# A gated attention and feed-forward block on one core: another order of the outer products, gated products through PSUM, stores by four, earlier inner factors of k and v, queued layernorms

## The chip, the cores and the metric

The kernel runs on one core of one Trainium2 chip, as one program with one launch. The metric is device time in microseconds. Three runs of the kernel before took 1561.82, 1562.58 and 1565.77 us; the median is 1562.58 us. One more execution was profiled. All shares and durations below are from it.

## The reference

Eight sequences of 512 tokens with 512 features go through one block in float32:

```python
xn = layernorm(x)                                    # (8, 512, 512)
q, k, v = xn @ Wq.T + bq, xn @ Wk.T + bk, xn @ Wv.T + bv
kv = cumsum((elu(k) + 1) * v, axis=tokens)
s  = ((elu(q) + 1) * kv * 32 ** -0.5) @ Wo.T + bo    # elementwise linear attention
h  = fwht(xn * SU_ug) / 64                           # normalized Walsh-Hadamard, 512
h  = silu(h @ W_gate.T * (Wscale_gate * 64)) * (h @ W_up.T * (Wscale_up * 64))   # 2048 wide
f  = (fwht(h * SU_dp) / 64) @ W_down.T * (Wscale_dp * 64)
out = x + s * silu(f)
```

The scan over tokens is elementwise per feature. The rest is matrix products, with the Hadamard transforms folded into the weights once, at the start.

## The kernel before

**Products.** Every large product is made by a fast scheme with seven products in place of eight for a matrix cut in two by two. The seven are called `P1` to `P7`; their factors are sums and differences of blocks of the tokens and of the weights. Most stages use it twice, one inside the other: an outer product is one of seven, and is itself made of seven inner ones. Inner products are accumulated in PSUM banks with the tags `px`, `py`, `pz` (3, 1 and 2 banks; two more have the tag `t`). After each step VectorE or ScalarE reads a partial sum out (`sa`, `sb`, `sc`) or adds a result (L737, L739, L743, L768, L770). TensorE goes on in the same bank only after the read.

**Pairs and stages.** The eight sequences are four pairs, `p` = 0 to 3. A pair has these stages, in order: attention (in pairs 0 and 1 from projected k, v and q; in pairs 2 and 3 k and v are made by outer products, `by_blocks`, L991), four hidden units `u` = 0 to 3 (`hidden_unit`, L1024), the output projection after unit 0 (`project_out`), the first half of the down product after unit 1, and its second half (`down`) after unit 3, with the gating, the residual and the output. The first half of down is `down` in pair 0 and seven outer products (`down_by_blocks`, L1093) in pairs 1 to 3. In time: pair 0 to about 451 us, pair 1 to 837, pair 2 to 1196, pair 3 to the end. Unit 1 and the outer products of down meet at about 640, 1010 and 1370 us.

**Hidden units.** One unit is seven outer products in the order `IN_TURN` = P1, P5, P6, P2, P7, P3, P4, each with its own weight tile `w_gu` from DRAM. Four results come out, numbered (a, s): (1,1) after the fifth outer product, (0,0), (0,1) and (1,0) later. `gated` turns a result into a gated product: ScalarE makes silu of the gate, an elementwise engine multiplies by the other lane, and subtractions make the factors that the down product needs (`ho`, seven places). In even units GpSimd does all of that, 1024 elements a partition at a time. In odd units (the ones before a down product) VectorE does it for (0,1) and (1,0). Subtractions are L1027, products L1035.

**Outer products of down.** For outer product `n` the function `factors` makes three inner factors from blocks of `ho` of units 0 and 1 (L1120 to L1122), and `last_factor` a fourth (L1129). GpSimd makes them, but for the second outer product, whose three are VectorE's. The order is `IN_TURN`. The results (`ra`, `rv`, `ru1`, `rr`, `u3`) are combined by `plus` (L1174). Each of the four is then transposed by VectorE in two pieces (L1148), into room in unit 1's `ho` that is no longer needed, and stored to DRAM in eight transfers of 64 KB (L1142). The order of weight loads follows the order of use; a list of all of them is written before the loop.

**What sets the order of work.** The program is written in steps of one inner factor. `at(n, fn)` puts work into an agenda, n steps from now; `advance` runs the agenda. `later(us, fn)` puts work into a queue called `idle`; `pace(ins, us)` takes work worth `us` from it whenever a result has been added, and places it behind that instruction on its engine. If a stage passes a time of zero, nothing is taken there. `catch_up` empties the queue. The framework then orders all instructions of each engine by its own plan. Every engine runs its own list in order. All loads and stores go through SP's queue, also in order. Weights are asked for three tiles ahead, from a pool of four.

**Buffers.** The pool `xin` has one buffer (tag `x`). It takes in turn a raw sequence for its layernorm, inner factors of down (`factors_down`, seven times in pair 1, every 13 steps from step 7) and the even sequence of the next pair's tokens (`squares`). Six buffers `t8` hold results, fetched sums and, in pair 1, the inner factors of k and v (`factors_kv`: four times two loads, seven stores and four additions or subtractions on VectorE), which begin after unit 1, in steps 2, 14, 26 and 38.

**Layernorms.** `normalized(b)` loads a sequence into `xin`, normalizes it and stores it. For b = 2 its 9 pieces are put into the queue. For b = 3 to 7 they are written as one block, at a lower priority (L148 statistics, L151 to L153 the root, L155 the scaling). In the profile, batch 4 is normalized at 551 to 573 us, 5 at 585 to 596, 6 at 823 to 832, 7 at 850 to 861.

Of the kernel before, what the change touches and what calls it, by code (L numbers as in the profile page):

```python
# [22 lines left out]
def kernel(  # L23
# [27 lines left out]
    nc = tc.nc  # L51
# [139 lines left out]
    def normalized(b):  # L191

        xt = load_x(b)
        d = dram.tile([L, D], F32, tag=f"d_x_{b}", name=f"d_x_{b}")
        kept[f"x_{b}"] = d

        def store():
            nc.sync.dma_start(d.rearrange("(n p) d -> p n d", p=P), xt)

        if b > 2:  # L200
            layernorm(b, xt)
            store()
# [241 lines left out]
    def factors_kv(m, lo, hi):  # L444
# [5 lines left out]
        t = t8.tile([P, 4, 4, P], F32, tag="t", name=f"f_{m}_{lo}")  # L450
# [573 lines left out]
    def hidden_unit(p, u, xo, ho, get_w, last, time=0):  # L1024
# [4 lines left out]
        def gated(t, a, s):  # L1029
            eng = nc.vector if last and a != s else nc.gpsimd  # L1030
            g, v = (t[:, :, lane].rearrange("p m q t -> p m (q t)") for lane in range(2))
            for m in range(2):
                nc.scalar.activation(g[:, m], g[:, m], AF.Silu, scale=col("w_gate", u + m * NU + a * NG))  # L1033
# [59 lines left out]
    def down_by_blocks(p, hos, get_w):  # L1093
# [15 lines left out]
        places = {}  # L1109

        def factors(n):
            o = IN_TURN[n]
            eng = nc.vector if n == 1 else nc.gpsimd
# [3 lines left out]
            else:  # L1117
                x, y = (block(0, q, IN_TURN[n - 3]) for q in range(2))
            b = block
            eng.tensor_tensor(x, b(1, 1, o), b(0, 1, o), ALU.subtract)  # L1120
            eng.tensor_tensor(b(0, 1, o), b(0, 1, o), b(0, 0, o), ALU.subtract)
            eng.tensor_tensor(y, b(1, 1, o), b(0, 1, o), ALU.subtract)  # L1122
# [4 lines left out]
        def last_factor(n):  # L1127
            b = block(1, 0, IN_TURN[n])
            nc.gpsimd.tensor_tensor(b, b, places[n][P6], ALU.subtract)  # L1129

        stored = []

        def turned(t, a, s):
            o = (P5, P1)[len(stored) // 2]
            z = h1[:, len(stored) % 2, o : o + 2]
            stored.append((a, s))

            def store():
                d = ds[s].rearrange("(i t) (c j f) -> j t c i f", t=32, j=4, f=32)
                for m in range(2):  # L1140
                    for j in range(4):
                        nc.sync.dma_start(  # L1142
                            d[j][:, 2 * a + m],
                            z[32 * j : 32 * j + 32, m].rearrange("p (i f) -> p i f", f=32),
                        )

            for m in range(2):
                at(1 + 2 * m, lambda m=m: nc.vector.transpose(z[:, m], t[:, m, 0].rearrange("p q t -> p (q t)")))  # L1148
            at(4, store)

        def outer(n, out, add=None, done=None):
            i = IN_TURN[n]
# [5 lines left out]
        u3, f0 = halves("u3")  # L1158
# [4 lines left out]
        at(3, lambda: factors(2))  # L1163
# [6 lines left out]
        ra, rv, ru1, rr, u3 = (result(t) for t in (ra, rv, ru1, rr, u3))  # L1170
# [5 lines left out]
        def with_u1():  # L1176
            plus(u3, ru1, rv)

        def with_r():
            plus(rv, rv, rr)  # L1180
# [184 lines left out]
    for p in range(B // 2):  # L1365
# [5 lines left out]
        for u in range(NU):  # L1371
# [7 lines left out]
            if u % 2:  # L1379
                if p and u == 1:  # L1380
                    queue += [(p, "dl", i) for i in IN_TURN]
# [112 lines left out]
    for p in range(B // 2):  # L1494
        if p:
            catch_up()
            inner_tokens(xo)
            if p == 1:
                for n, i in enumerate(IN_TURN):
                    at(7 + 13 * n, lambda i=i: factors_down(i))  # L1500
            co = hop.tile([P, 2, 7, L], F32, tag="h", name=f"co_{p}")
# [3 lines left out]
        for u in range(NU):  # L1505
# [9 lines left out]
            else:  # L1515
# [8 lines left out]
                hidden_unit(p, u, xo, ho, get_w, u % 2 == 1, 1.1 if p > 1 and u == 0 else 0)  # L1524
# [8 lines left out]
            if u == 1:  # L1533
# [12 lines left out]
        flush()  # L1546
        ds = [fetch(f"d_{p}_{s}") for s in range(2)]
# [59 lines left out]
```

## Time and profile before

| | |
|---|---|
| median of three runs | 1562.58 us (1561.82 to 1565.77) |
| profiled execution: its time, and its span from the first to the last instruction | 1559.57 us, 1557.8 us |
| TensorE busy | 1507.0 us, 97% of the span, 6008 matmuls |
| VectorE busy | 1143.8 us, 73% |
| ScalarE busy | 408.0 us, 26% |
| GpSimd busy | 472.0 us, 30% |
| granted TensorE clock, mean | 0.994 |
| DMA | 307.31 MB, mean 197 GB/s |

PE is TensorE, PEld its weight loads, DVE VectorE, ACT ScalarE, POOL GpSimd, SP the engine that issues the DMAs; "SPq" is its sequencer. Lnnn is a line of the kernel. A group or a row has the line, the engine, the operation, output and input by the program's names, the shape, and how many. In square brackets stand the idle time of the engine before it and what ended that idle time. The ends of matmuls are modelled and overlap, so a busy TensorE is not one at its peak. Starts are in us from the start of the span.

### The profile page before, as it was taken

How to read it: one execution, taken by the hardware profiler on the slowest of the kernel's cores; microseconds unless marked ns; L12 is line 12 of the kernel's file. 1: busy time of each engine (PE TensorE's matmuls, PEld its weight loads, DVE VectorE, ACT ScalarE, POOL GpSimd, SP SyncE). 2: the span in 40 equal slices, each digit the busy share in tenths (PEclk: the TensorE clock that was granted, in tenths of full speed). 3: DMA queues.
4: the chain of work that ended last, by engine and by line, in shares of the span. 5: the costliest groups of instructions: out<-in, count | busy, mean ns of one | idle time of the engine just before them, and what ended most of it. 6: DMA issues, size and time to landing. Idle time of an engine off the chain costs nothing.

```text
span 1557.8 us, 16546 instructions
## 1 busy us (share of the span) xinstructions
PE 1507.0 (97%) x6008; PEld 1139.2 (73%) x6008; DVE 1143.8 (73%) x1743; ACT 408.0 (26%) x668; POOL 472.0 (30%) x263
## 2 busy tenths in 40 slices
PE   7998999999999989888999999999999999989998
PEld 3446446748864778777886888878887788878887
DVE  8999787569756876876677796676675697576673
ACT  4462341232134321201214332111211432111211
POOL 1000000001211261843622227471622118381731
PEclk9999999999999999999999999999999999999999
DMA  9346878798956656698586643548475342538472
GB/s 278 94 141 175 260 269 239 226 306 286 267 173 212 235 179 213 199 271 235 178 248 228 188 150 135 180 127 197 168 230 189 121 161 97 200 136 197 157 259 83
DMA packets 274481, 307.31 MB, mean 197 GB/s; under 512 B 108640, under 2 KB 227680, under 8 KB 271712
## 3 DMA queue, kind: packets, MB, share of 16 engines
q1 hardware_dynamic: 274256, 306.22, 63.5%
q8 instruction: 47, 0.77, 0.2%
q14 instruction: 34, 0.28, 0.1%
q10 hardware_dynamic: 144, 0.03, 0.0%
HBM read 217.35 MB, written 88.87 MB: 197 GB/s over the span
## 4 chain that ended last, share of the span: by engine, by line
PE 71%; DVE 14%; DMA 4%; POOL 3%; SPq 3%; issue 2%; ACT 2%; POOLq 0%; DVEq 0%; ACTq 0%
PE px_gu L713 13%; PE px_dn L616 7%; PE pz_gu L713 6%; PE py_gu L713 3%; PE pz_dn L616 3%; PE px_q L540 3%; PE px_kv L713 3%; PE px_o L616 3%; PE px_gate L540 2%; PE px_dl L722 2%; PE py_dn L616 2%; PE px_up L540 2%; PE pz_o L616 2%; PE pz_kv L713 2%; PE px_k L540 1%
## 5 line engine op out<-in xcount | busy, mean ns | idle before, releaser
L713 PE MATMUL px_gu<-xo,w_gu 128*128 128x256 f32 x1456 | 350.6, 381 | 11.2 <-DMA w_gu<-d_gu 6.8
L713 PEld LDWEIGHTS px_gu<-xo,w_gu 128*128 128x128 f32 x1456 | 275.7, 190 | 57.2 <-DMA w_gu<-d_gu 6.3
L1005 POOL TENSOR_TENSOR u_gu<-u_gu,v_gu 128x1024 f32<-128x1024 f32 x26 | 61.2, 2373 | 630.7 <-DVE u_gu L770 569.7
L713 PE MATMUL pz_gu<-xo,w_gu 128*128 128x256 f32 x728 | 189.9, 384 | 1.9 <-DVE u_gu L743 1.8
L713 PEld LDWEIGHTS pz_gu<-xo,w_gu 128*128 128x128 f32 x728 | 139.2, 192 | 23.3 <-DVE u_gu L743 3.8
L616 PE MATMUL px_dn<-w_down,ho 128*128 128x256 f32 x640 | 143.0, 379 | 1.8 <-DVE ho L94 1.8
L616 PEld LDWEIGHTS px_dn<-w_down,ho 128*128 128x128 f32 x640 | 121.5, 190 | 20.3 <-DVE ho L94 2.2
L713 PE MATMUL py_gu<-xo,w_gu 128*128 128x256 f32 x364 | 95.1, 383 | 0.0
L1062 POOL TENSOR_TENSOR s<-s,d 128x512 f32<-128x512 f32 x30 | 39.4, 1312 | 166.4 <-ACT d L1061 166.4
L722 PE MATMUL px_dl<-ho,w_dl 128*128 128x256 f32 x300 | 75.1, 386 | 3.0 <-ACT sc_dl L737 1.4
L713 PEld LDWEIGHTS py_gu<-xo,w_gu 128*128 128x128 f32 x364 | 69.5, 191 | 9.6 <-DVE v_gu L743 0.2
L616 PE MATMUL pz_dn<-w_down,ho 128*128 128x256 f32 x304 | 69.1, 379 | 0.6 <-DVE u L556 0.6
L722 PEld LDWEIGHTS px_dl<-ho,w_dl 128*128 128x128 f32 x300 | 57.2, 193 | 14.0 <-ACT sc_dl L737 2.6
L1009 POOL TENSOR_TENSOR v_gu<-v_gu,r_gu 128x1024 f32<-128x1024 f32 x26 | 60.9, 2363 | 18.2 <-DVE r_gu L770 18.2
L616 PEld LDWEIGHTS pz_dn<-w_down,ho 128*128 128x128 f32 x304 | 57.5, 190 | 10.3 <-issue 1.2
L540 PE MATMUL px_q<-xo,w_q 128*128 128x512 f32 x128 | 59.8, 593 | 0.0
L616 PE MATMUL px_o<-w_o,co 128*128 128x256 f32 x256 | 59.2, 380 | 0.3 <-DVE sa_o L627 0.3
L1061 ACT ACTIVATE d<-d 128x512 f32<-128x512 f32 x31 | 19.5, 630 | 148.8 <-DVE d L631 126.4
L1027 POOL TENSOR_TENSOR ho<-ho 128x1024 f32<-128x1024 f32 x24 | 56.6, 2367 | 1.4
L737 ACT COPY sa_gu<-px_gu 128x512 f32<-128x512 f32 x26 | 15.1, 581 | 157.9 <-PE px_gu L713 129.1
L1033 ACT ACTIVATE a_gu<-a_gu,cols_sb 128x512 f32<-128x512 f32 x26 | 18.6, 720 | 141.6 <-DVE a_gu L770 140.2
L616 PEld LDWEIGHTS px_o<-w_o,co 128*128 128x128 f32 x256 | 48.3, 190 | 8.9 <-issue 1.0
(373 smaller groups left out, 2833.9 us busy)
## 6 DMA issues: line engine op xcount, KB each, us to landing
w_gu<-d_gu SPq DMA_DIRECT2D x91, 896.0 KB, 4.7
w_dl<-d_dl SPq DMA_DIRECT2D x21, 896.0 KB, 4.5
w_down<-d_down SPq DMA_DIRECT2D x35, 512.0 KB, 5.3
w_kv<-d_kv SPq DMA_DIRECT2D x14, 896.0 KB, 4.7
d_s<-o SPq DMA_DIRECT2D x8, 1024.0 KB, 6.2
d<-d_d SPq DMA_DIRECT2D x8, 1024.0 KB, 6.1
s<-d_s SPq DMA_DIRECT2D x8, 1024.0 KB, 8.3
y<-in_x_dram SPq DMA_DIRECT2D x8, 1024.0 KB, 6.8
```

The lines of the kernel that those rows point to most:

```text
L540: nc.tensor.matmul(p.rearrange("p a t -> p (a t)") if len(r.shape) == 2 else p, ws[k][:, i, :], r, start=(first and k == 0), stop=(k == n ...
L616: nc.tensor.matmul(p[:, c], t[:, (2 * g + c) * P : (2 * g + c + 1) * P], ws[i](k), start=(first and k == 0 and c == cs[0]), stop=(k == n - ...
L713: nc.tensor.matmul(p[:, lane], w[:, lane, i, :], x[:, i, :], start=(first and lane == 0), stop=True, skip_group_check=True,)
L722: nc.tensor.matmul(p[:, 0], w[:, k, i, :], x(k, i), start=(first and k == 0), stop=(k == 1), skip_group_check=True,)
L737: nc.scalar.copy(s, px)
L1005: nc.gpsimd.tensor_tensor(r[:, m], ru1[:, m], rv[:, m], ALU.add)
L1009: nc.gpsimd.tensor_tensor(rv[:, m], rv[:, m], rr[:, m], ALU.add)
L1027: eng.tensor_tensor(ho[:, :, c], ho[:, :, a], ho[:, :, b], ALU.subtract)
L1033: nc.scalar.activation(g[:, m], g[:, m], AF.Silu, scale=col("w_gate", u + m * NU + a * NG))
L1061: nc.scalar.activation(d, d, AF.Silu)
L1062: (nc.vector if final and (a, s) == (1, 0) else nc.gpsimd).tensor_tensor(r, r, d, ALU.mult)
```

## The change

It has six parts.

- **Gated products of odd units.** For (0,1) and (1,0) ScalarE writes silu of the gate into a PSUM bank of the tag `t`, in two pieces of 512 elements. VectorE multiplies there, and forms P5 and P7 (or P2) from the PSUM piece. GpSimd does the two remaining subtractions, P6 and P4.
- **Order of the outer products of down**: P1, P3, P6, P5, P7, P2, P4 in place of `IN_TURN`. All `factors` are GpSimd's, all `last_factor` VectorE's. The result `r3` takes the place of `u3`: it is the second outer product, and two sums are added to it later.
- **Turned results.** The eight transposes of a pair go into the queue. Each sequence is stored once, in four transfers of 256 KB, when both its results are there.
- **Inner factors of k and v** begin in steps 100, 114, 128 and 142 of pair 1, which is in unit 0 and `project_out`, and use the buffer `xin`.
- **Layernorms** of b = 4 to 7 are put into the queue, from step 12 after unit 1 or 2; b = 3 is still a block.
- **Pacing.** Hidden units of pairs 1 to 3 take work from the queue (1.1 us for a result), but for unit 0 of pair 1. Before, only unit 0 of pairs 2 and 3 did. At the end of a pair the queue is emptied.

```diff
-        if b > 2:
+        if b == 3:
             layernorm(b, xt)
...
-        t = t8.tile([P, 4, 4, P], F32, tag="t", name=f"f_{m}_{lo}")
+        t = xin.tile([P, 3, 7, P], F32, tag="x", name=f"f_{m}_{lo}")
+        t = t.rearrange("p c s e -> p (c s e)")[:, : 16 * P].rearrange("p (a s e) -> p a s e", a=4, s=4)
...
         def gated(t, a, s):
-            eng = nc.vector if last and a != s else nc.gpsimd
+            eng = nc.gpsimd
             g, v = (t[:, :, lane].rearrange("p m q t -> p m (q t)") for lane in range(2))
+            if last and a != s:
+                bs = []
+                for m in range(2):
+                    b = bank("t", f"g_{p}_{u}_{a}_{m}", 1)[:, 0]
+                    nc.scalar.activation(b, g[:, m], AF.Silu, scale=col("w_gate", u + m * NU + a * NG))
+                    if s:
+                        nc.vector.tensor_tensor(b, b, v[:, m], ALU.mult)
+                        nc.vector.tensor_tensor(ho[:, m, P5], b, ho[:, m, P1], ALU.subtract)
+                        bs.append(b)
+                    else:
+                        nc.vector.tensor_tensor(ho[:, m, P2], b, v[:, m], ALU.mult)
+                if s:
+                    sub(eng, P6, P3, P5)
+                    for m in range(2):
+                        nc.vector.tensor_tensor(ho[:, m, P7], ho[:, m, P3], bs[m], ALU.subtract)
+                else:
+                    sub(eng, P4, P2, P6)
+                return
...
+        ORDER = (P1, P3, P6, P5, P7, P2, P4)
...
-            eng = nc.vector if n == 1 else nc.gpsimd
...
-            eng.tensor_tensor(x, b(1, 1, o), b(0, 1, o), ALU.subtract)
+            nc.gpsimd.tensor_tensor(x, b(1, 1, o), b(0, 1, o), ALU.subtract)
...
         def last_factor(n):
-            b = block(1, 0, IN_TURN[n])
-            nc.gpsimd.tensor_tensor(b, b, places[n][P6], ALU.subtract)
+            b = block(1, 0, ORDER[n])
+            nc.vector.tensor_tensor(b, b, places[n][P6], ALU.subtract)
...
         def turned(t, a, s):
...
-            for m in range(2):
-                at(1 + 2 * m, lambda m=m: nc.vector.transpose(z[:, m], t[:, m, 0].rearrange("p q t -> p (q t)")))
-            at(4, store)
+            z = h1[:, s, 2 * a : 2 * a + 2]
+            for m in range(2):
+                later(0.7, nc.vector.transpose, z[:, m], t[:, m, 0].rearrange("p q t -> p (q t)"))
+
+        def store(s):
+            z = h1[:, s, 0:4].rearrange("p c (i f) -> p c i f", f=32)
+            d = ds[s].rearrange("(i t) (c j f) -> j t c i f", t=32, j=4, f=32)
+            for j in range(4):
+                nc.sync.dma_start(d[j], z[32 * j : 32 * j + 32])
...
-        def with_u1():
-            plus(u3, ru1, rv)
...
+        def with_v():
+            plus(r3, r3, rv)
+            plus(r3, r3, ru1)
+
+        def with_a():
+            turned(r3, 0, 1)
             turned(rv, 1, 1)
+            later(0.0, store, 1)
+            turned(ra, 0, 0)
+
+        def with_c():
+            turned(ru1, 1, 0)
+            later(0.0, store, 0)
...
         outer(0, ra)
-        outer(1, rv)
-        outer(2, ru1, ra, with_u1)
-        outer(3, ra, ra, lambda: turned(ra, 0, 0))
-        outer(4, rr, ru1, with_r)
-        outer(5, u3, u3, lambda: turned(u3, 0, 1))
-        outer(6, ru1, rr, lambda: turned(ru1, 1, 0))
+        outer(1, r3)
+        outer(2, ru1, ra)
+        outer(3, rv, None, with_v)
+        outer(4, rr, ru1, lambda: plus(rv, rv, rr))
+        outer(5, ra, ra, with_a)
+        outer(6, ru1, rr, with_c)
...
+                for i, (m, lo, hi) in enumerate((("k", 0, 4), ("k", 4, 7), ("v", 0, 4), ("v", 4, 7))):
+                    at(100 + 14 * i, lambda m=m, lo=lo, hi=hi: factors_kv(m, lo, hi))
...
-                hidden_unit(p, u, xo, ho, get_w, u % 2 == 1, 1.1 if p > 1 and u == 0 else 0)
+                hidden_unit(p, u, xo, ho, get_w, u % 2 == 1, 1.1 if p and (p > 1 or u) else 0)
...
-                if p == 1:
-                    for i, (m, lo, hi) in enumerate((("k", 0, 4), ("k", 4, 7), ("v", 0, 4), ("v", 4, 7))):
-                        at(2 + 12 * i, lambda m=m, lo=lo, hi=hi: factors_kv(m, lo, hi))
...
+        if p:
+            catch_up()
```

More of the change, by code (lines that the diff above doesn't have):

```diff
@@ L1109, in down_by_blocks @@
         places = {}
+        ORDER = (P1, P3, P6, P5, P7, P2, P4)
         def factors(n):
-            o = IN_TURN[n]
-            eng = nc.vector if n == 1 else nc.gpsimd
+            o = ORDER[n]
             if n < 3:
@@ L1117, in factors @@
             else:
-                x, y = (block(0, q, IN_TURN[n - 3]) for q in range(2))
+                x, y = (block(0, q, ORDER[n - 3]) for q in range(2))
             b = block
-            eng.tensor_tensor(x, b(1, 1, o), b(0, 1, o), ALU.subtract)
-            eng.tensor_tensor(b(0, 1, o), b(0, 1, o), b(0, 0, o), ALU.subtract)
-            eng.tensor_tensor(y, b(1, 1, o), b(0, 1, o), ALU.subtract)
+            nc.gpsimd.tensor_tensor(x, b(1, 1, o), b(0, 1, o), ALU.subtract)
+            nc.gpsimd.tensor_tensor(b(0, 1, o), b(0, 1, o), b(0, 0, o), ALU.subtract)
+            nc.gpsimd.tensor_tensor(y, b(1, 1, o), b(0, 1, o), ALU.subtract)
             places[n] = {
@@ L1127, in last_factor @@
         def last_factor(n):
-            b = block(1, 0, IN_TURN[n])
-            nc.gpsimd.tensor_tensor(b, b, places[n][P6], ALU.subtract)
-        stored = []
+            b = block(1, 0, ORDER[n])
+            nc.vector.tensor_tensor(b, b, places[n][P6], ALU.subtract)
         def turned(t, a, s):
[L1134 to L1139, printed above, removed]
-                for m in range(2):
[L1141 to L1145, printed above, removed]
-            for m in range(2):
-                at(1 + 2 * m, lambda m=m: nc.vector.transpose(z[:, m], t[:, m, 0].rearrange("p q t -> p (q t)")))
-            at(4, store)
+            z = h1[:, s, 2 * a : 2 * a + 2]
+            for m in range(2):
+                later(0.7, nc.vector.transpose, z[:, m], t[:, m, 0].rearrange("p q t -> p (q t)"))
[4 more added lines that the diff above has]
+                nc.sync.dma_start(d[j], z[32 * j : 32 * j + 32])
         def outer(n, out, add=None, done=None):
-            i = IN_TURN[n]
+            i = ORDER[n]
             w = get_w("dl", i)
@@ L1156, in outer @@
             )
-        u3, f0 = halves("u3")
+        r3, f0 = halves("r3")
         room.append(f0)
@@ L1162, in down_by_blocks @@
         at(0, lambda: factors(1))
-        at(3, lambda: factors(2))
+        at(2, lambda: factors(2))
         for n in range(3, 7):
@@ L1169, in down_by_blocks @@
         ru1, rr = halves("u1")
-        ra, rv, ru1, rr, u3 = (result(t) for t in (ra, rv, ru1, rr, u3))
+        ra, rv, ru1, rr, r3 = (result(t) for t in (ra, rv, ru1, rr, r3))
         def plus(o, a, b):
@@ L1174, in plus @@
             nc.vector.tensor_tensor(o, a, b, ALU.add)
-        def with_u1():
-            plus(u3, ru1, rv)
-        def with_r():
-            plus(rv, rv, rr)
-            turned(rv, 1, 1)
-        outer(0, ra)
-        outer(1, rv)
-        outer(2, ru1, ra, with_u1)
-        outer(3, ra, ra, lambda: turned(ra, 0, 0))
-        outer(4, rr, ru1, with_r)
-        outer(5, u3, u3, lambda: turned(u3, 0, 1))
-        outer(6, ru1, rr, lambda: turned(ru1, 1, 0))
+        def with_v():
[3 more added lines that the diff above has]
+            turned(r3, 0, 1)
+            turned(rv, 1, 1)
+            later(0.0, store, 1)
[3 more added lines that the diff above has]
+            later(0.0, store, 0)
+        outer(0, ra)
+        outer(1, r3)
[4 more added lines that the diff above has]
+        outer(6, ru1, rr, with_c)
         between()
@@ L1380 @@
                 if p and u == 1:
-                    queue += [(p, "dl", i) for i in IN_TURN]
+                    queue += [(p, "dl", i) for i in (P1, P3, P6, P5, P7, P2, P4)]
                 else:
```

## The prediction

> **What bounds the kernel now.** I read the summary first, then busy time by stretches, then the order of time inside the bad stretches, on each engine.
>
> ```profile
> span 1557.8 us, 16546 instructions
> PE 1507.0 (97%) x6008; PEld 1139.2 (73%) x6008; DVE 1143.8 (73%) x1743; ACT 408.0 (26%) x668; POOL 472.0 (30%) x263
> ```
>
> ```profile
> 540.00:580.00 40.00, 34.27 (x147) 28.87 (x146) 31.53 (x46) 9.61 (x12) 28.25 (x12) 0.91 0.57 194
> 640.00:690.00 50.00, 43.75 (x189) 34.93 (x190) 45.80 (x70) 4.15 (x9) 34.96 (x22) 1.00 0.82 255
> 690.00:726.00 36.00, 29.20 (x117) 23.88 (x116) 16.83 (x29) 4.00 (x7) 4.66 (x2) 0.91 0.97 245
> 726.00:775.00 49.00, 49.00 (x229) 43.14 (x228) 33.51 (x50) 11.58 (x18) 30.42 (x13) 1.00 0.57 186
> 1000.00:1045.00 45.00, 41.42 (x178) 34.03 (x177) 33.82 (x47) 6.86 (x14) 39.42 (x26) 0.96 0.38 124
> 1360.00:1405.00 45.00, 40.02 (x178) 32.80 (x177) 34.36 (x48) 6.86 (x14) 39.50 (x26) 1.00 0.37 123
> ```
>
> TensorE is the bound; the change alters no product, so it can only win back gaps. In the chain of waits eight 128x256 matmuls take 1.73 us, 0.216 us each. A stretch (columns: length; busy and instructions of PE, PEld, DVE, ACT, POOL; clock; DMA share; GB/s) loses its length less 0.216 times its matmuls: A, 540 to 580, 40 - 147 x 0.216 = 8.2 us; B, 640 to 690, 9.2; C, 690 to 726, 10.7; D, 1000 to 1045, 6.6; E, 1360 to 1405, 6.6. Together 41.3. The undisturbed 726 to 775 comes out at 49.5 for 49, so the method is good to half a us. B, D and E are the outer products of pairs 1, 2, 3.
>
> A, in time order:
>
> ```profile
> 565.65 7.38 POOL L1027 TENSOR_TENSOR ho<-ho 128x1024 f32<-128x1024 f32 x3
> 566.38 6.93 DVE L155 TENSOR_SCALAR x<-x,mv,rstd 128x512 f32<-128x512 f32 x3
> 574.56 3.78 PE L616 MATMUL pz_o<-w_o,co 128*128 128x256 f32 x8 [5.32 <-DVE u_gu L743]
> ```
>
> The scaling of batch 4 runs in one block beside POOL; three take 6.93 us, where the median of that line's 20 is 0.54 each. Evictions queue behind, TensorE waits 5.3 us, and then runs eight matmuls in 3.78 instead of 1.73: the granted clock (0.91 in A and C) charges a long stop twice.
>
> E (D and B begin alike):
>
> ```profile
> 1369.62 2.25 DVE L1035 TENSOR_TENSOR ho<-u_gu 128x1024 f32<-128x1024 f32 x1 [1.81 <-ACT u_gu L1033]
> 1374.13 3.10 DVE L1027 TENSOR_TENSOR ho<-ho 128x1024 f32<-128x1024 f32 x2
> 1372.53 1.13 PE L713 MATMUL px_gu<-xo,w_gu 128*128 128x256 f32 x4 [1.13 <-DVE sc_gu L739]
> 1379.29 1.13 PE L722 MATMUL py_dl<-ho,w_dl 128*128 128x256 f32 x4 [1.01 <-DVE a_dl L743]
> 1388.50 1.10 PE L722 MATMUL pz_dl<-xy_dl,w_dl 128*128 128x256 f32 x4 [1.01 <-DVE a_dl L743]
> ```
>
> Seven waits of 0.38 to 1.13 us, nearly all for evictions behind VectorE work of 1.2 to 3.1 us.
>
> C:
>
> ```profile
> 681.52 8.15 SPq L1142 DMA_DIRECT2D d_d<-ho  x8
> 697.02 1.13 PE L713 MATMUL px_gu<-xo,w_gu 128*128 128x256 f32 x4 [2.68 <-DMA w_gu<-d_gu]
> 707.43 1.13 PE L713 MATMUL px_gu<-xo,w_gu 128*128 128x256 f32 x4 [2.41 <-DMA w_gu<-d_gu]
> 390.55 17.06 SPq L243 DMA_DIRECT2D z<-d_x  x8
> ```
>
> Weights come late since SP issues 32 result stores and most of the 36 transfers of k's and v's factors there. Pairs 2 and 3 issue the 32 stores without the factors and do not stop.
>
> **The change part by part.**
>
> *Gated products through PSUM* (every odd unit). Gone from VectorE in E: 2.25 + 1.21 + 3.10 + 2.17 + 2.17 = 10.9 us in blocks. Added: eight 128x512 operations with a PSUM operand; the evictions with one (L743) take 0.68 beside a busy POOL, so 5.4. ScalarE does as many silu as before, 0.72 each. POOL gets two subtractions at 2.36 = 4.7. The third factor (P6) now waits for POOL: its subtraction needs P5 and the (1,1) product, done at 1370.8 in E, so it ends about 1373.5; factors take 3 x 1.27, so P6's are ready near 1381 in today's clock, and its outer product's first use is about 1384. Cover: 3 us; without it, up to 2.4 us (one subtraction) a pass.
>
> *Order and engines of the factors.* Second is now P3, from the product ready earliest, in place of P5. Three operations leave VectorE (1.75 + 1.42 + 1.16 = 4.3) for POOL (3.8), seven last factors go the other way: POOL loses 8.9, VectorE gains 7 x (0.67 alone to 1.4 contended, the 128x512 rows of f_k and f_v) = 4.7 to 9.8. I take 7: POOL is busy 39.5 of 45. One more 128x1024 sum costs 1.2 to 1.9, one outer product fewer adds while evicting (4 x 0.41 off VectorE, 4 x 0.36 on ScalarE). POOL's total changes by 4.7 + 3.8 - 8.9 = -0.4, VectorE's by 5.4 + 7 + 1.5 - 10.9 - 4.3 - 1.6 = -2.9. What counts is that the longest blocks fall from 3.1 to 1.4, or two sums in a row (3 to 4) once. In E a block of 2.25 cost a wait of 1.13, so about 1.1 is free and 1.4 costs 0.3. I leave 1.5 us a pass: the 0.46 for ScalarE with 0.16 to refill, and three times 0.3. Ends: 0, or 4 if the sums, last factors and POOL's order all show.
>
> *Layernorms queued.* Batch 4 leaves A. Its statistics (4 x 0.84) and scalings go between evictions of the outer products in B, batch 6's in D (it cost nothing in the second half of pair 1's down, at 822), 5's and 7's into unit 3 (5's costs nothing now, in project_out at 585). A scaling beside POOL: 0.54 to 2.56, so four are 2.2 to 10.2. B and D have POOL busy 35 of 50 and 39 of 45, nearest the contended end, but its operations there are 1.27 rather than 2.46, so I take 1.8 each, 7.2 in all, in pieces; PE pays 2 us in B and in D (ends 0 and 6), 0.3 in each unit 3 (ends 0 and 2).
> The Trainium skill, "SBUF — State Buffer", section "Who interferes with whom", speaks against this move: a VectorE operation in a two-port mode, or with two SBUF inputs, is shut out for the whole of a GpSimd instruction. By it each scaling waits out one 1.27 us operation, 1.8 with its own 0.54; the row of A, taken as it stands, gives 2.56, and 3 us more of VectorE a pass. The rows of A agree in direction.
>
> *k's and v's factors sooner, in the input buffer.* All 36 transfers leave B and C for unit 0 and project_out of pair 1; so do 16 encodings (0.54 to 1.42 us, some 16 us). Unit 0 has no pacing there, so they start in project_out, where evictions need 14 x 0.68 of 24 us. A keeps 1.0 (ends 0 and 5). Four fills of one buffer, about 12 us each as pair 1's down factors show (521 to 531, 531 to 544), end near 610, 40 us before batch 4 is due. SP's waits for these encodings stand ahead of unit 1's weights, which land 4.5 to 7 us before use: 1.0 (ends 0 and 4).
>
> *Stores by four.* 32 stores of 64 KB become 8 of 256 KB with the same 128-byte runs, in two groups queued behind transposes. Bounds: eight loads of this very shape held SP 17.06 us in one burst; the old groups hold it 6 to 8 us four times, and in pair 2 cut the weights' lead from 7.4 us to 3.0 without a stop. If both groups go in a row, a weight load is up to 17 late and stops PE 10 us a pass; with a load between them 8.5 - 7.4 = 1.1. I take 1.5 a pass, nearer the second, since the second group waits for another outer product. In C this replaces 10.7; in D and E it is new.
> The transposes now wait for a paced eviction; only the stores stand behind them, and d_d is read some 80 us later.
> The Trainium skill, "DMA: Bandwidth & Descriptors", section "Rules for kernel authors", would coalesce, calling transfers under 64 KB mostly overhead: by it three quarters of the queue time would go, an estimate of 20 of 27 us. The rows say 10: 17 for eight of this shape against four groups of 6 to 8.
>
> *Batches 5 and 7 stored later.* Their input buffer is needed for the next tokens, so eight loads (17 us of SP) fall at the end of unit 3, as for pair 0 now at 390 to 407, where the later wait, at 413, is 0.15, 0.3 with the refill. Pair 0's `down` starts on three of four terms, the others on two, so I charge 0.7 twice (ends 0 and 10).
>
> Sum: A 8.2 - 1.0 = 7.2; weights in unit 1 -1.0; B 9.2 - 3.5 = 5.7; C 10.7 - 1.5 = 9.2; D 6.6 - 5.0 = 1.6; E 6.6 - 3.0 = 3.6; unit 3 -0.6; ends -1.4. Gain 24.3. The profiled execution took 1559.57 (span 1557.8): 1535.3. The runs' median is 3.0 above it: 1538.
>
> **The rivals.** (1) Late weights: both store groups hold SP in a row and PE stops 6 us a pass instead of 1.5: 1538 + 13.5 = 1552. For: 17.06. Against: a 7.4 us lead. (2) POOL becomes the bound: factors late by one subtraction a pass (3 x 2.4), and the evictions keep two thirds of the old waits (2.5 a pass more): 1538 + 7.2 + 7.5 = 1553. For: POOL at 88% in D and E; against: its total falls. (3) Slower: the one input buffer. It now carries seven down factors, four kv factors, two batches and the next tokens one after another. If batch 5 (and 7) is stored late, the next pair's tokens and the down weights queued behind their loads hold PE at the end of pairs 1 and 2. Beyond about 9 us before unit 3's end each us costs one us a pass; 12 us a pass too late eats the gain, 15 gives 1538 + 30 = 1568. Against: the queue empties by the fifth outer product of seven, some 12 us before the end. (4) Little changes: the order shifts, and only C's gain stays, half of it eaten: 1558 to 1562.
>
> **How the numbers follow.** Forecast 0.62, (1) 0.13, (2) 0.12, (3) 0.08, (4) 0.05. The likeliest is 1538. Taking the low ends of all new costs gives 1562.6 - 41.3 = 1521, which is not likely as a whole: low 1524; (1) and (2) are held: high 1556. No change means within 0.3% (4.7 us), what a measurement here can tell. Faster 0.87 (forecast, (1), (2)), same 0.05, slower 0.08.
>
> **What would show it.** Right: no VectorE block over 2 us at the start of B, D, E; no wait of PE for batch 4's scaling; d_d as 24 transfers and no PE wait for w_gu after B; f_k and f_v before 620. Wrong: PE waits for w_gu after each outer-product stage, for POOL's factors, or for w_down or tokens at the ends of pairs 1 and 2.

## The result, and the profile after

The changed kernel takes 1587.33 us (median of four runs, 1586.74 to 1589.24), the kernel before 1564.17 beside it (four runs). The ratio is 1.0149, with an interval of 1.0127 to 1.0171: slower by 1.5%. The forecast was 1538 us and faster, with a range up to 1556.

The profiled execution took 1589.24 us. Its summary:

```profile
span 1587.4 us, 16472 instructions
PE 1513.7 (95%) x6008; PEld 1146.7 (72%) x6008; DVE 1124.2 (71%) x1760; ACT 413.1 (26%) x680; POOL 477.3 (30%) x265
```

The same 6008 matmuls, VectorE 20 us less busy and GpSimd 5 us more. The forecast said 9 less and 1 less, over three passes (a pass is the seven outer products of down of one pair). No engine has become the bound by its total. The time is in waits. The stretches where it is lost (columns: length; busy time and instructions of PE, PEld, DVE, ACT, POOL; granted clock; DMA share; GB/s):

```profile
556.00:586.00 30.00, 24.67 (x99) 20.55 (x99) 19.52 (x21) 4.22 (x6) 22.16 (x9) 0.89 0.54 176
600.00:622.00 22.00, 14.27 (x57) 11.53 (x56) 6.87 (x12) 3.52 (x6) 0.00 (x0) 0.84 0.96 319
648.00:690.00 42.00, 34.83 (x151) 28.98 (x150) 30.23 (x54) 8.97 (x19) 31.11 (x22) 0.96 0.50 166
712.00:742.00 30.00, 25.19 (x102) 21.05 (x101) 15.78 (x24) 3.90 (x5) 6.62 (x3) 0.89 0.76 198
1388.00:1420.00 32.00, 26.27 (x120) 22.08 (x119) 18.66 (x33) 6.95 (x15) 30.48 (x21) 1.00 0.35 115
1452.00:1478.00 26.00, 20.45 (x82) 16.95 (x81) 12.44 (x20) 2.03 (x3) 4.94 (x3) 0.87 0.71 187
```

By length less 0.216 us a matmul they lose 8.6, 9.7, 9.4, 8.0, 6.1 and 8.3 us. In the kernel before, the second stretch, 600 to 622, has PE busy for all of its 22 us:

```profile
600.00:622.00 22.00, 22.00 (x104) 19.36 (x103) 13.45 (x21) 4.24 (x7) 4.68 (x2) 1.00 0.86 268
```

For the whole span I add up, over all matmuls, the time from one start to the next beyond 0.216 us (0.429 for 512 columns). That counts waits and slow-clocked matmuls together. It gives 60.3 us before and 89.7 after: 29.4 more, where the spans differ by 29.6. The medians differ by less, 23.2 us: the profiled execution before was faster than each of its four runs, the one after the slowest of its four. By place:

| loss, us | before | after | forecast of the difference |
|---|---|---|---|
| `project_out`, pair 1 (A) | 8.6 | 8.9 | -7.2 |
| unit 1, pair 1: weights late | 0 | 9.9 | +1.0 |
| outer products, pairs 1, 2, 3 (B, D, E) | 10.2, 7.0, 6.9 | 9.9, 10.4, 6.5 | -13.9 in all |
| weights late after them, pairs 1, 2, 3 | 11.2, 0, 0 | 8.3, 7.8, 8.7 | -6.2 in all |
| the rest | 16.4 | 19.3 | +2.0 |
| sum | 60.3 | 89.7 | -24.3 |

The last column splits the forecast's terms by place: the passes are B, D and E without the stores (3.5 - 9.2, 3.5 - 6.6, 1.5 - 6.6), the weights after them are C and three times 1.5 (4.5 - 10.7). Of the rest's 2.9 us more, 1.6 lie in pair 0, whose loss varies by itself: from 10.7 to 15.2 us between the change and those runs below that leave its pair 0 alone. So differences of a few us between whole losses say little, and those by place more.

What PE waits for, after (us in total, times, longest):

```profile
PE px_gu L714 <- DMA w_gu<-d_gu: 23.9, 7, 7.7
PE px_dl L723 <- DVE sb_dl L740: 11.7, 3, 4.3
...
PE px_dl L723 <- POOL xy_dl L1141: 5.3, 3, 1.8
PE pz_o L617 <- DVE u_gu L744: 4.1, 1, 4.1
PE px_gu L714 <- DVE sc_gu L740: 2.5, 3, 0.8
```

Before, the same view had these in their place:

```profile
PE px_gu L713 <- DMA w_gu<-d_gu: 6.8, 3, 2.7
PE pz_o L616 <- DVE u_gu L743: 5.3, 1, 5.3
PE px_gu L713 <- DVE sc_gu L739: 3.7, 4, 1.1
```

So many short waits were exchanged for a few long ones, of two kinds: weights (23.9 us in place of 6.8), and one eviction a pass (11.7 us), which is new. Each has a cause that a timeline shows.

**Weights after the outer products.** SP's queue at the end of pair 3's pass, and what PE does then (start, duration, line; idle time before it in brackets):

```profile
1442.90 6.08 SPq L1159 DMA_DIRECT2D d_d<-ho  x4
1449.09 2.24 SPq L346 DMA_DIRECT2D w_gu<-d_gu  x1
1451.43 8.55 SPq L1159 DMA_DIRECT2D d_d<-ho  x4
1460.09 3.22 SPq L346 DMA_DIRECT2D w_gu<-d_gu  x3
```

```profile
1456.58 1.13 PE L714 MATMUL px_gu<-xo,w_gu 128*128 128x256 f32 x4 [0.40 <-DMA w_gu<-d_gu]
...
1468.03 2.05 PE L714 MATMUL px_gu<-xo,w_gu 128*128 128x256 f32 x4 [5.14 <-DMA w_gu<-d_gu]
```

The eight stores and one weight load take 16.9 us of SP, in which PE uses up nearly three weight tiles (one every 6.05 us). By that cadence the two loads were due at 1443.25 and 1449.30. They were issued 5.8 and 10.8 us late and landed 7.4 to 7.8 us after issue. The first costs 0.40 us, the second 5.14 and slow matmuls behind it, the first four in 2.05 us in place of 1.13.

**The eviction.** VectorE, GpSimd and PE in pair 3's pass:

```profile
1411.48 1.74 DVE L1148 TENSOR_TENSOR ho<-ho,xy_dl 128x512 f32<-128x512 f32 x1 [6.90 <-POOL ho L1028]
1413.14 0.41 DVE L740 TENSOR_TENSOR sb_dl<-px_dl,a_dl 128x256 f32<-128x256 f32 x1
```

```profile
1396.08 2.81 POOL L1028 TENSOR_TENSOR ho<-ho 128x1024 f32<-128x1024 f32 x1
...
1405.44 1.26 POOL L1141 TENSOR_TENSOR xy_dl<-ho,ho 128x512 f32<-128x512 f32 x1
...
1409.11 2.34 POOL L1028 TENSOR_TENSOR ho<-ho 128x1024 f32<-128x1024 f32 x1
```

```profile
1406.75 1.13 PE L723 MATMUL px_dl<-xy_dl,w_dl 128*128 128x256 f32 x4 [1.76 <-POOL xy_dl L1141]
...
1413.61 1.13 PE L723 MATMUL px_dl<-ho,w_dl 128*128 128x256 f32 x4 [3.13 <-DVE sb_dl L740]
```

L1148 is P6's last factor, now VectorE's. It overwrites P6's block of unit 1 in place. GpSimd's subtraction for P4 (`sub(eng, P4, P2, P6)`, at 1409.11) still has to read that block. VectorE executes in order, so it stands for 6.90 us, and the eviction behind it holds PE for 3.13 (4.3 in pairs 1 and 2). The row at 1396.08 is P6's own subtraction. The P5 that it needs is complete at 1393.53, but P3's factors run first on GpSimd; after it, factors of P5 and P7 run between those of P6, and P6's last comes at 1406.70, when PE had waited 1.76 us.

**A and unit 1.** VectorE and GpSimd in `project_out` of pair 1:

```profile
564.40 2.33 DVE L466 TENSOR_TENSOR f_k<-f_k 128x512 f32<-128x512 f32 x1
...
570.61 4.39 DVE L466 TENSOR_TENSOR f_k<-f_k 128x512 f32<-128x512 f32 x2
```

```profile
566.26 8.19 POOL L1028 TENSOR_TENSOR ho<-ho 128x1024 f32<-128x1024 f32 x3
```

k's encodings (the additions and subtractions that make its inner factors) have taken the place of batch 4's scalings beside the same three subtractions, at 2.2 us each. PE waits 4.12 us there, against 5.32 before. At 600 us SP's queue holds seven factor stores ahead of a weight load:

```profile
600.80 1.51 SPq L459 DMA_DIRECT2D d_kv<-f_v  x3
...
604.95 4.02 SPq L459 DMA_DIRECT2D d_kv<-f_v  x4
609.07 0.81 SPq L346 DMA_DIRECT2D w_gu<-d_gu  x1
```

PE when that load has landed:

```profile
616.02 2.08 PE L714 MATMUL px_gu<-xo,w_gu 128*128 128x256 f32 x4 [7.73 <-DMA w_gu<-d_gu]
```

The kernel before issued the same load at 594.26, 14.8 us sooner.

### The profile page after: what moved, and what is told of

Same layout as the page of the kernel before. It is cut to its first block, busy times and chain, and to the rows that moved or that the text cites. A ratio compares the mean times of both kernels' runs of the same rounds, so it can differ in the third digit from the quotient of the medians.

```text
span 1587.4 us, 16472 instructions
## 1 busy us (share of the span) xinstructions
PE 1513.7 (95%) x6008; PEld 1146.7 (72%) x6008; DVE 1124.2 (71%) x1760; ACT 413.1 (26%) x680; POOL 477.3 (30%) x265
## 4 chain that ended last, share of the span: by engine, by line
PE 70%; DVE 11%; POOL 7%; DMA 7%; issue 3%; SPq 2%; ACT 1%; POOLq 0%; DVEq 0%; ACTq 0%
PE px_gu L714 13%; PE px_dn L617 7%; PE pz_gu L714 6%; PE py_gu L714 3%; DMA w_gu<-d_gu 3%; PE pz_dn L617 3%; PE px_kv L714 3%; PE px_dl L723 3%; PE px_q L541 3%; PE px_o L617 3%; PE px_gate L541 2%; PE py_dn L617 2%; PE px_up L541 2%; PE pz_kv L714 2%; PE pz_dl L723 1%
## 5 line engine op out<-in xcount | busy, mean ns | idle before, releaser
L714 PE MATMUL px_gu<-xo,w_gu 128*128 128x256 f32 x1456 | 354.7, 384 | 27.1 <-DMA w_gu<-d_gu 23.9
L1028 POOL TENSOR_TENSOR ho<-ho 128x1024 f32<-128x1024 f32 x38 | 91.7, 2421 | 24.9 <-DVE ho L1043 14.7
L723 PE MATMUL px_dl<-ho,w_dl 128*128 128x256 f32 x300 | 75.2, 386 | 12.0 <-DVE sb_dl L740 11.7
L1010 POOL TENSOR_TENSOR v_gu<-v_gu,r_gu 128x1024 f32<-128x1024 f32 x26 | 60.9, 2363 | 16.4 <-DVE r_gu L771 14.3
L617 PEld LDWEIGHTS pz_dn<-w_down,ho 128*128 128x128 f32 x304 | 57.4, 190 | 10.8 <-issue 1.2
L1082 DVE TENSOR_TENSOR y<-y,s 128x512 f32<-128x512 f32 x31 | 21.4, 691 | 51.2 <-POOL s L1081 51.0
```

The lines of the kernel that those rows point to most:

```text
L617: nc.tensor.matmul(p[:, c], t[:, (2 * g + c) * P : (2 * g + c + 1) * P], ws[i](k), start=(first and k == 0 and c == cs[0]), stop=(k == n - ...
L714: nc.tensor.matmul(p[:, lane], w[:, lane, i, :], x[:, i, :], start=(first and lane == 0), stop=True, skip_group_check=True,)
L723: nc.tensor.matmul(p[:, 0], w[:, k, i, :], x(k, i), start=(first and k == 0), stop=(k == 1), skip_group_check=True,)
L1010: nc.gpsimd.tensor_tensor(rv[:, m], rv[:, m], rr[:, m], ALU.add)
L1028: eng.tensor_tensor(ho[:, :, c], ho[:, :, a], ho[:, :, b], ALU.subtract)
L1082: nc.vector.tensor_tensor(y, y, r, ALU.add)
```

## The experiments

Ratios are against the kernel before, run beside each on the same chip, with the 95% interval. "Loss" is the sum of the whole span, 60.3 before and 89.7 after. The medians of the kernel before lie between 1560.72 and 1564.17 us from one set of runs to another, so times of different sets are compared by their ratios, and a difference of a few us between two ratios is not told apart from noise.

**e1: the old stores.** The change, with the turned results collected and stored as before (`r3`, `rv`, `ra`, `ru1` after the outer products 3 to 6):

```diff
+            for m in range(2):
+                at(1 + 2 * m, lambda m=m: nc.vector.transpose(z[:, m], t[:, m, 0].rearrange("p q t -> p (q t)")))
+            at(4, store)
...
-        outer(4, rr, ru1, lambda: plus(rv, rv, rr))
-        outer(5, ra, ra, with_a)
-        outer(6, ru1, rr, with_c)
+        outer(4, rr, ru1, with_r)
+        outer(5, ra, ra, lambda: turned(ra, 0, 0))
+        outer(6, ru1, rr, lambda: turned(ru1, 1, 0))
```

> The changed kernel with the turned results handled as before: each of the four results is transposed a few steps after it is complete and stored at once in eight transfers of 64 KB, four groups an outer product apart. Theory 1 (the two groups of four large stores hold SP's queue in a row, and the weights behind them land late): the waits for w_gu after the outer products of pairs 1, 2 and 3 (8.3, 7.7 and 8.6 us with their slow clock) go, 1587 - 22 = 1565 us, 1560 to 1570. Rival (the traffic of 128-byte runs on the DMA engines delays the weights, however it is cut): the same 16384 runs a pass still delay them, 1580 or more.

1565.1 us, 1.0033 (1.0018 to 1.0048), loss 65.8. PE's waits for `w_gu` fall from seven to one, the one in unit 1. SP's queue of this kernel at the same place:

```profile
1427.20 6.42 SPq L1161 DMA_DIRECT2D d_d<-ho  x8
1433.72 0.45 SPq L346 DMA_DIRECT2D w_gu<-d_gu  x1
1434.27 6.18 SPq L1161 DMA_DIRECT2D d_d<-ho  x8
```

Here too the groups follow one another with one weight load between them, but a group of this size holds the queue for 6.2 to 6.4 us and the load for 0.45, so the next load follows 6.8 us later. In the change the loads at 1437.21, 1449.09 and 1460.09 are 11.9 and 11.0 us apart, against a cadence of 6.05. The stores are worth 18 us by the two ratios and 24 by the losses, the largest single part.

**e2: a gap between the two groups.**

```diff
-            later(0.0, store, 0)
+            later(0.0, at, 14, lambda: store(0))
```

> The changed kernel with one thing different: the second group of four large stores is issued 14 steps (two outer products, 12 us) later. Theory 1: each group alone delays the next weight by about 6 us, which the lead of 7.4 us just covers, so most of the waits for w_gu after the outer products go: 1587 - 18 = 1569 us, 1563 to 1575. Rival (it is the size of one transfer or the small runs, not that the groups follow one another): one group is enough to stop PE, 1580 or more.

1566.8 us, 1.0039 (1.0025 to 1.0053), loss 67.2. The large stores are kept and cost nearly nothing, with 14 steps between the groups:

```profile
1427.67 6.09 SPq L1159 DMA_DIRECT2D d_d<-ho  x4
1433.87 6.56 SPq L346 DMA_DIRECT2D w_gu<-d_gu  x3
1440.52 10.21 SPq L1159 DMA_DIRECT2D d_d<-ho  x4
```

The second group holds the queue even longer (10.21 us). So one group of large stores alone does not stop PE, and by e1 neither do groups of small ones in a row: in these runs it takes two large groups with only one load between them.

**e3: k's and v's factors back** to their own buffers and to steps 2, 14, 26, 38 after unit 1.

```diff
-        t = xin.tile([P, 3, 7, P], F32, tag="x", name=f"f_{m}_{lo}")
+        t = t8.tile([P, 4, 4, P], F32, tag="t", name=f"f_{m}_{lo}")
...
+                        at(2 + 12 * i, lambda m=m, lo=lo, hi=hi: factors_kv(m, lo, hi))
```

> The changed kernel with the inner factors of k and v where they were: in a t8 buffer, in steps 2 to 38 after unit 1 of pair 1. Theory 2 (their encodings beside POOL's subtractions hold PE in project_out of pair 1, and SP's waits for them make a weight of unit 1 late): the 8 us at 570 to 583 fall to 1 and the 10 us at 608 to 620 go, while the crowd on SP after unit 1 comes back and meets the large stores, 8 us turning into some 16: 1587 - 7 - 10 + 8 = 1578 us, 1572 to 1585. Rival (the stretch 570 to 583 has another cause, the pacing of unit 0's end): it stays, 1585 or more.

1576.27 us, 1.0097 (1.008 to 1.0114), loss 76.9. The losses in A and in unit 1 are gone; after pair 1's outer products 8.8 us stay, as without this edit.

**e4: P6's last factor on GpSimd.**

```diff
-            nc.vector.tensor_tensor(b, b, places[n][P6], ALU.subtract)
+            (nc.gpsimd if n == 2 else nc.vector).tensor_tensor(b, b, places[n][P6], ALU.subtract)
```

> The changed kernel with one of the seven last factors, that of P6 (third outer product), back on POOL; six stay on VectorE. Theory 3 (this one overwrites the P6 block that POOL's subtraction for P4 has still to read, so VectorE stands still for it, and the evictions behind it): the waits of 4.3, 4.3 and 3.1 us in the outer products of pairs 1, 2 and 3 go with their slow clock, 1587 - 14 = 1573 us, 1569 to 1578; the wait of 1.8 us for POOL's factor just before stays. Rival (VectorE and POOL hinder each other at the ports, whichever holds this factor): 1584 to 1590.

1578.72 us, 1.0124 (1.0103 to 1.0144), loss 78.3. All three waits for `sb_dl` go, so the factor's place behind GpSimd is their cause. The time alone does not show the gain: 8.6 us by the medians, but 3.9 by the ratios, whose intervals overlap. The passes lose 18.8 us in place of 26.8, so 8.0 are gained there (3.4 of the loss's 11.4 lie in pair 0). About 14 were expected. In pairs 1 and 2 a wait came to light that the old one had covered: that for the four queued scalings, which stand in a row on VectorE.

```profile
1029.66 5.98 DVE L219 TENSOR_SCALAR x<-x,mv,rstd 128x512 f32<-128x512 f32 x4
```

PE waits 2.4 us for the eviction behind them (`sc_dl`, at 1035.56). In pair 3, without a layernorm, PE waits 2.2 for GpSimd's factor itself.

**e5: k's and v's factors in unit 2 of pair 1**, in `t8`, steps 14, 28, 42, 56.

```diff
+                            at(14 + 14 * i, lambda m=m, lo=lo, hi=hi: factors_kv(m, lo, hi))
```

> The changed kernel with one thing different: the inner factors of k and v are made in unit 2 of pair 1 (t8 buffer, steps 14, 28, 42 and 56 after the outer products), where neither project_out's evictions nor the stores of the outer products are. Theory 2 (it is their place in unit 0 and project_out that costs 8.9 us at 570 to 582 and 9.9 us at 616 to 620): both go and 2 us come new in units 2 and 3, 1587 - 17 = 1570 us, 1565 to 1576. Rival (the 36 transfers and 16 encodings hold PE wherever they are): the loss only moves, 1582 or more.

1586.36 us, 1.0159 (1.0143 to 1.0174), loss 86.7: a miss by 16 us, and the rival held. The loss in A and unit 1 moved along with the work, to 702 to 771 us and to the down weights at 805. The waits of PE in this kernel:

```profile
PE px_gu L713 <- DMA w_gu<-d_gu: 15.7, 6, 5.4
...
PE py_dn L616 <- DMA w_down<-d_down: 4.0, 2, 3.2
PE py_gu L713 <- DVE v_gu L743: 3.0, 2, 2.8
```

**e6: the three together** (old stores, factors in unit 2, P6's last factor on GpSimd).

> The changed kernel with three things different together: the turned results stored as before, the inner factors of k and v in unit 2 of pair 1, the last factor of P6 on POOL. Theories 1, 2 and 3 name the whole loss, and the three are independent: 1587 - 22 - 17 - 8 = 1540 us, 1535 to 1546, below the kernel before. Rival (the three share one cause, or the time shifts into a new wait): 1550 or more.

1556.86 us, 0.9965 (0.9948 to 0.9981), loss 58.2. Faster than before, but 17 us short, and the rival's range: its profile loses 19.0 us between 690 and 840 us, where the factors of k and v now are. The kernel before loses 11.1 there.

**e7: gated products through PSUM alone**, in the kernel before.

```diff
-            eng = nc.vector if last and a != s else nc.gpsimd
+            eng = nc.gpsimd
...
+                    nc.scalar.activation(b, g[:, m], AF.Silu, scale=col("w_gate", u + m * NU + a * NG))
```

> The kernel before with one part of the change alone: the gated products of odd units through PSUM. The prediction's step (shorter VectorE blocks at the start of the outer products): of 7.0, 7.0 and 6.9 us some 3 stay in each pass, 1561 - 11 = 1550 us, 1545 to 1555. Rival (POOL's two subtractions more make its factors late by as much as VectorE wins): 1558 to 1564.

1561.04 us, 1.0000 (0.9987 to 1.0013), loss 62.3: a miss. VectorE at the start of pair 3's pass:

```profile
1374.66 0.68 DVE L1046 TENSOR_TENSOR ho<-ho,t_g 128x512 f32<-128x512 f32 x1
1375.26 2.52 DVE L1138 TENSOR_TENSOR xy_dl<-ho,ho 128x512 f32<-128x512 f32 x1
1377.70 0.68 DVE L739 TENSOR_TENSOR sc_gu<-px_gu,r_gu 128x512 f32<-128x512 f32 x1
```

Six pieces of 0.7 from 1371.46 on (the last is shown) and a factor stand in a row ahead of the eviction `sc_gu`. PE waits 3.2 us once, 5.2 with the slow clock, in place of seven short waits that made 7.0. Shorter instructions in an unbroken row hold an eviction as long ones do, but the longest part of this row is the factor, 2.52 us, which the change gives to GpSimd. In the change the same six pieces stand there without it, and PE waits 0.8 us for `sc_gu` in each pass.

**e8: queued layernorms alone**, in the kernel before.

```diff
-        if b > 2:
+        if b == 3:
...
-                hidden_unit(p, u, xo, ho, get_w, u % 2 == 1, 1.1 if p > 1 and u == 0 else 0)
+                hidden_unit(p, u, xo, ho, get_w, u % 2 == 1, 1.1 if p and (p > 1 or u) else 0)
```

> The kernel before with one part of the change alone: the layernorms of batches 4 to 7 queued, with the pacing that serves the queue. Theory 4: the 7.7 us at 575 to 579 go, but the scalings of batches 4 and 6, 1.5 to 1.8 us each beside POOL, stop PE some 2.7 us in the outer products of pairs 1 and 2, and the late stores of batches 5 and 7 cost about 1 us each at the ends of pairs 1 and 2: 1561 - 8 + 7 = 1560 us, 1556 to 1563. Rival (the prediction's price, 2 us, or less since the pieces lie between evictions): 1552 to 1556.

1567.76 us, 1.0040 (1.0026 to 1.0054), loss 68.5, above the range. A's 8.6 us go, but 3.2 come in pair 1's outer products, 5.6 in pair 2's, 5.0 in the weights after pair 1's and 1.7 in pair 1's `down`. VectorE in pair 1's pass:

```profile
654.23 5.04 DVE L219 TENSOR_SCALAR x<-x,mv,rstd 128x512 f32<-128x512 f32 x4
```

**e9: the subtractions for P6 and P4 on VectorE**, in the change.

```diff
-                    sub(eng, P6, P3, P5)
+                    sub(nc.vector, P6, P3, P5)
...
-                    sub(eng, P4, P2, P6)
+                    sub(nc.vector, P4, P2, P6)
```

> The changed kernel with the two subtractions of odd units that the change gave to POOL (P6 and P4, 128x1024) on VectorE as before; their products still go through PSUM. Theory 3 (POOL makes P6 too late for its factors, and P4 too late for VectorE's last factor of P6): the waits of 1.8 us for POOL's factor and of 4.3, 4.3 and 3.1 us behind the last factor go in all three passes, 23 us with refill and slow clock; the queued scalings come to light, some 3 us in pairs 1 and 2: 1587 - 23 + 6 = 1570 us, 1564 to 1577. Rival (VectorE's blocks of 1.2 to 2.2 us come back and hold the evictions as before): 1580 or more.

1584.44 us, 1.0150 (1.0135 to 1.0166), loss 84.1: a miss, in the rival's range, and by the ratio no gain. The two waits it was aimed at shrink, from 1.8 to 0.7 and from 4.3 to 0.8 us. A wait for `sc_gu` grows to 2.5 in each pass, since a subtraction of 1.82 us now follows the six pieces, and the scalings' wait shows (2.0, in pairs 1 and 2). The last factor stays on VectorE here, so what held the evictions was its wait for GpSimd's subtraction, and not that VectorE makes it.

**e11: only the scalings moved to ScalarE**, in the kernel before (b = 3 to 7).

```diff
-                nc.vector.tensor_scalar(
-                    xt[:, i + t, :], xt[:, i + t, :], mv[:, t, 0:1], rstd[:, t : t + 1],
-                    ALU.subtract, ALU.mult,
+                nc.scalar.activation(
+                    xt[:, i + t, :], xt[:, i + t, :], AF.Identity, bias=nmr[:, t : t + 1], scale=rstd[:, t : t + 1]
```

> The kernel before with one thing different: the four scalings of each layernorm block (batches 3 to 7) on ScalarE, with one small operation more on VectorE. Theory 4 (the 7.7 us at 575 to 579 come from scalings on VectorE that POOL shuts out, 2.56 us in place of 0.54): 1561 - 7.5 = 1554 us, 1550 to 1557. Rival (what holds PE there is POOL's or ScalarE's work on unit 0's last result, whatever normalizes): 1559 to 1563.

1555.15 us, 0.9960 (0.9948 to 0.9973), loss 55.1. ScalarE takes 0.73 us for one beside the same GpSimd work, where VectorE took 2.3, and the wait of 5.32 is gone:

```profile
566.99 2.93 ACT L157 ACTIVATE x<-x,nmr,rstd 128x512 f32<-128x512 f32 x4 [1.96 <-DVE nmr L155]
```

**e12: no encodings.** The change, without the 16 additions and subtractions for k's and v's factors.

```diff
-            nc.vector.tensor_tensor(t[:, o, :n], t[:, x, :n], t[:, y, :n], op)
             store(c, o)
```

> The changed kernel without the 16 additions and subtractions of k's and v's inner factors; all 36 transfers stay, and unencoded blocks are stored, so k and v of pairs 2 and 3 are not the reference's. Theory 2, sharper (VectorE's encodings, beside POOL, hold PE at 570 to 582, and SP standing for each of them makes the weight at 616 late): 8.9 falls to 1 and 9.9 to 3, 1587 - 15 = 1572 us, 1568 to 1577. Rival (the transfers themselves and their waits for one another hold SP): 570 to 582 goes, 616 stays, 1577 to 1582.

1583.83 us, 1.0141 (1.0124 to 1.0157), loss 87.2: above both ranges. It separates the two losses of that part. A falls from 8.9 to 1.0, so A's is VectorE's. The wait in unit 1 stays and even grows, to 9.23 us, so it comes from the transfers in SP's queue and not from VectorE. Another 2.5 us of waits for `w_down` appear at the end of pair 2, and the whole loss falls by only 2.5. PE in this kernel:

```profile
607.25 2.08 PE L713 MATMUL px_gu<-xo,w_gu 128*128 128x256 f32 x4 [9.23 <-DMA w_gu<-d_gu]
```

**e10: what is left, put together.** The change's order of outer products, VectorE's last factors and the gated products through PSUM, with e9's subtractions; stores, place of k's and v's factors, and pacing as before; the layernorms of b = 3 to 7 as blocks, with e11's scalings.

> A kernel from what the runs have shown: order of the outer products, factors and gated products as in the change, but the two subtractions on VectorE, the stores, the place of k's and v's factors and the pacing as before, and the layernorms of batches 3 to 7 in one block as before with the four scalings on ScalarE in place of VectorE. If theories 1 to 4 hold, of the loss of 60 us before some 17 in pair 0, 1 at 575, 4, 2 and 2 in the outer products and 11 after those of pair 1 stay: 1561 - 23 = 1538 us, 1532 to 1547. Rival (ScalarE, which also evicts and makes silu, becomes late with the scalings, or the subtractions hold VectorE): 1550 to 1560.

1546.29 us (1544.81 to 1548.41), 0.9902 (0.9889 to 0.9916), loss 45.9: faster than both kernels. A and unit 1 in this kernel, same columns as above:

```profile
556.00:586.00 30.00, 30.00 (x140) 26.17 (x139) 20.82 (x39) 11.41 (x15) 20.42 (x9) 1.00 0.46 161
600.00:622.00 22.00, 22.00 (x104) 19.36 (x103) 16.36 (x25) 3.31 (x4) 9.34 (x5) 1.00 0.65 187
```

PE does not stop in either. Most of what is left of the passes is the wait for `sc_gu`, 2.5 us in each; 6.7 us of waits for weights after pair 1's stay.

## Why the prediction was wrong

The direction was wrong. The forecast gain was 24.3 us, the loss 29.4 in the profile (23.2 by the medians); the 53.7 between them come from five terms of the sum.

**Stores by four: 19.8 us.** The prediction had the mechanism, as rival (1), and even a bound of 10 us a pass. It took 1.5, "nearer the second, since the second group waits for another outer product". That step failed: the second group came 2.4 us after the first with one load between. One load is not enough for groups this long, since they and the load take 16.9 us of SP, nearly three weight tiles; in e1 two groups and the load take 13.25, and it is enough. Measured: 7.8 to 8.7 a pass, above even the rival's 6, for the wait takes the slow clock with it. In pair 1 that replaced 11.2 us, in pairs 2 and 3 it is new. The rule weighed in the prediction (the Trainium skill, "DMA: Bandwidth & Descriptors", section "Rules for kernel authors": coalesce) is about what the transfers cost in all, and there it holds in direction. In pair 3 the same 2 MB held SP for 5.93, 5.08, 6.42 and 6.27 us before, 23.7 in all, and for 6.08 and 8.55 after, 14.6. So 9 us were saved, close to the prediction's 10 from the rows, and half of the 20 that it estimated by the page. But PE does not wait for the total; it waits when a weight load stands behind a group that holds the queue too long.

**Outer products: 16.6 us.** Forecast -13.9, measured +2.7. Two steps failed; by place they make 17.0 and 5.8 of the 26.8 us that the passes lose.
- "Seven last factors go the other way" was priced as durations on VectorE (4.7 to 9.8). A moved instruction takes its waits along. P6's waits for GpSimd's reader of the block it overwrites, and every eviction behind it waits too: 17.0 us with the slow clock in the three passes; e4 takes those waits away.
- P6's factors were to be ready with a cover of 3 us. PE waited 1.8 for them: GpSimd ran P6's subtraction 2.5 us after its inputs were there, behind P3's factors, and then factors of P5 and P7 ahead of P6's last. The price without cover, up to 2.4 a pass, was right: 2.0, since each of these waits loses 0.16 us more than its length.

The step on the shorter blocks held: 1.5 us were left for the evictions at the start of a pass, and the change loses 1.1 there (the wait for `sc_gu`). It does so together with the other order and GpSimd's factors; alone, in e7, the gated products gain nothing (0.9987 to 1.0013).

**Unit 1's weights: 8.9 us.** Priced at 1.0 with ends of 0 and 4; 9.9 measured. The step that failed is the lead: "weights, which land 4.5 to 7 us before use", against a load issued 14.8 us later than before. Loads and stores of the factors stand in the in-order queue ahead of the weights, and wait for each other there (SP waits 5.4 us for a load of v to land and 3.4 for stores of k). e12 shows that the encodings are not needed for that. Whether the one buffer is, remains open: e5, with the six of `t8`, loses 14.7 us where it puts them, but that is another stage.

**A: 7.5 us.** "A keeps 1.0 (ends 0 and 5)": 8.9. The prediction priced the scalings beside GpSimd's long subtractions and then moved other VectorE operations, with two SBUF inputs, into the same place, with 0.54 to 1.42 us from rows beside shorter GpSimd work. They take 2.2. The rule that it had cited for the layernorms (the Trainium skill, "SBUF — State Buffer", section "Who interferes with whom": a VectorE operation with two SBUF inputs contends with GpSimd) applies to these as well and was not asked. e11 and e12 agree with it from both sides: without the scalings, or without the encodings, A loses 1.4 and 1.0 us.

**The rest: 0.9 us.** Rival (3), late tokens at the ends of pairs, did not come: the changed kernel waits 0.5 us for `w_down` in all, and that in pair 0. So the 2.0 us priced for unit 3 and the ends did not come either; what came in their place is mostly pair 0's.

**Right in size:** a scaling in the queue takes 1.2 to 1.5 us where 1.8 was said. The four were to run "in pieces", but stand in a row; why isn't shown. In the change the wait for `sb_dl` covers them; in e4 they cost PE a wait of 2.4 a pass where 2 was said, and e8 loses 3.2 to 5.6 more a pass in the other order of instructions. The layernorms' move out of A does take the scalings' wait away, but alone it costs more than that elsewhere (1.0040). Rival (2), GpSimd as the bound, holds for its place and not for its total: its busy time hardly changes, and what stops PE is the order of its list.

What remains open: e10 keeps the change's order and adds e11's scalings; of its gain of 15 us over the kernel before, e11 alone has 6.2. How the other nine divide between order, last factors and gated products wasn't tried.

## What to carry to other kernels

When an instruction moves to another engine, list what it must wait for, in-place overwrites included, and then what stands behind it in that engine's order; its duration was the smaller part of its price here. For transfers ask not how much a queue carries but for how long it carries nothing else, and compare that with the cadence of the loads behind it. Before an operation is moved into a stage, look at what ran badly there before: here the same neighbour did the same to the newcomer.

## What the runs showed of the hardware

- A wait can cost more than itself: the granted clock falls to half for a few us behind it (0.50 from 1016 to 1019 us in the kernel before). In the changed kernel it was 0.84 to 0.89 in four of the six bad stretches, and waits of 4 to 8 us were charged with 1.6 to 3.1 us more. After the wait of 7.73 us four matmuls took 2.08 us, as after 5.14 (2.05).
- The length of a wait does not settle it. The wait of 3.13 us in pair 3's pass is the same in the change and in e1; the four matmuls behind it took 1.13 us in the change (row at 1413.61) and 1.68 in e1, where those after them are slow too. In the kernel before, the same short waits of 1.13 and 0.60 us were followed by slow matmuls in pair 2 and not in pair 3. The first two rows are e1's, the others those of the kernel before:

```profile
1396.59 1.68 PE L723 MATMUL px_dl<-ho,w_dl 128*128 128x256 f32 x4 [3.13 <-DVE sb_dl L740]
1398.06 1.91 PE L723 MATMUL py_dl<-ho,w_dl 128*128 128x256 f32 x4
```

```profile
1015.50 1.80 PE L713 MATMUL pz_gu<-xo,w_gu 128*128 128x256 f32 x4 [0.60 <-DVE u_gu L743]
...
1374.26 1.13 PE L713 MATMUL pz_gu<-xo,w_gu 128*128 128x256 f32 x4 [0.60 <-DVE u_gu L743]
```

  The Trainium skill, "TensorE: Matmul & The Clock Gate", Part 1, puts the fall to half rate after an idle window of about 3.4 us. The waits over 4 us agree with it. The slow rows behind shorter waits, 3.13 and 0.60 us, do not fit a rule by the length of one wait, and what decides there is not shown.
- Four stores of 256 KB (1 MB) held SP's queue for 6.08, 8.55, 6.09 and 10.21 us, eight of 64 KB (0.5 MB) for 6.18 and 6.42.
- A scaling or a difference of 512 elements took VectorE 0.5 to 0.8 us alone, 1.2 to 1.5 beside mostly short GpSimd operations (1.3 to 2.4 us), and 2.2 to 2.3 beside its 1024-wide ones; a scaling on ScalarE, 0.73 beside the same.
